# The ninth tap of a split-float32 convolution: 64-row matmuls side by side, or one full-array matmul

## The chip, the cores and the metric

The kernel runs on one core of one Trainium2 chip. The metric is the device time of one execution in microseconds (us); the time before is the median of three runs. A core has TensorE (PE in the profile, with PEld for its weight loads), VectorE (DVE), ScalarE (ACT), GpSimd (POOL) and SyncE (SP). ACT and SP also issue the DMAs of this kernel.

## The reference, cut to what matters

Three layers of one kind, then a fourth of another. `_gn` is a group norm without parameters.

```python
def _L0_conv_ref(inputs, M, Wp, G):          # B,H,W,C = 4,32,32,16; G: (32,32,3,3,16,16)
    first = jnp.einsum('ijpq,bpqc->bijc', M2, inputs)
    K = jnp.transpose(G, (2, 3, 4, 0, 1, 5)).reshape(kh, kw, c, h * w * f)
    shifted = lax.conv_general_dilated(inputs, K, (1, 1), 'SAME', ...)
    shifted = shifted.reshape(b, h, w, h, w, f)
    diff = jax.nn.relu(inputs[:, :, :, None, None, :] - shifted)
    second = jnp.einsum('ijpq,bpqijc->bijc', W2, diff)
    return first - second

x = x + _L0_conv_ref(_gn(x), ...)            # likewise layers 1 and 2
x = x + _L3_conv_ref(_gn(x), ...)            # a 2-D convolution with an impulse response
```

So each layer convolves four 32x32 images of 16 channels with 16384 filters of 3x3x16, one set of 16 filters per output position, subtracts, clips, and sums over all positions with a weight. The convolution is nearly all of the work.

## The kernel before, in words

**Operands.** The products are wanted at float32 accuracy, and PE takes a float32r operand in one pass. Every operand is therefore split exactly into a high piece rounded to float32r and a low remainder, and the four products of the pieces are summed in PSUM. `load_patches` makes `main[0]` (high) and `main[1]` (low): 128 partitions that hold eight of the nine taps times 16 channels, for two image pairs. `load_g` makes `gh` and `gl` of the same 128 rows of the filters. Filters come in 16 chunks per layer, each of `GC` = 8 blocks of 128 columns; a block is 8 output positions times 16 channels.

**The ninth tap** has only 16 rows. `last` holds them eight times over, high and low by turns, and `gn` holds the filters' 16 rows eight times, high in rows 0 to 31 and 64 to 95, low in the others. Rows 0 to 63 thus contain all four products once, and rows 64 to 127 contain them again. Two 64-row matmuls with different images, on the upper and the lower half of the array, each do the whole ninth tap.

**Loops.** A job is one block and one image pair; a layer has 256 jobs. The first 16 take the eight blocks of chunk 0 with pair 0 and then with pair 1; later ones take both pairs of a block in turn. Jobs go two at a time (L311): `main_taps` of the first (16 matmuls of 128 rows and 512 columns, L277), `last_tap` of both (four 64-row matmuls each, L289), `main_taps` of the second. So the array changes between full and 64-row matmuls twice per pair of jobs. A job accumulates into two PSUM tiles of two banks (`pair_psum`, four buffers, all of PSUM). VectorE then takes each tile in one instruction (L301): minimum with zero, times the weights `w`, summed into `acc`.

**Supply.** `next_g` loads the next chunk's filters at the third block of a chunk. ACT issues the DMA of `g` and the eight copies of `g9`, and casts `gh` (L234) and `gn` (L236). POOL subtracts the identity from the middle tap of `g` (L225). VectorE computes `gl` (L235) and the low rows of `gn` (L239, twice). `g` and `g9` have one buffer, `gh`, `gl` and `gn` two, so a chunk's casts wait until PE is through with the chunk two before. SP loads `w`, 1 MB for two blocks, four buffers deep (L254).

**A layer's start.** Group norm on VectorE, `ypad` to DRAM (L140) and back as shifted patches (L158, L167), on SP and ACT by turns; then the first term (L192) with eight loads of `M` (L178), three buffers deep. In layer 0 the impulse response of the last convolution follows on PE, ACT and POOL (L350 to L396). The order of instructions on each engine is set by the framework's scheduler, which also gives each DMA one of eight completion lanes in turn; a DMA waits for the one before it on its lane. [...]

Of the kernel before, what the change touches and what calls it, by code (L numbers as in the profile page):

```python
# [23 lines left out]
F32 = mybir.dt.float32  # L28
F32R = mybir.dt.float32r
AF = mybir.ActivationFunctionType  # L30
ALU = mybir.AluOpType
# [5 lines left out]
B, C, S = 4, 16, 32  # L37
# [3 lines left out]
GC = 8  # L41
# [8 lines left out]
def conv_stack_kernel(ctx, tc, x, M, W, G, den, num, h0, cst, dft, idft, out):  # L50
    nc = tc.nc
# [14 lines left out]
    def pair_psum():  # L66
        return ps.tile([P, 2, 512], F32, tag="pt", name="pt")
# [24 lines left out]
    def group_norm(xt):  # L92

        s = small.tile([P, B], F32, tag="s", name="s")
        nc.vector.tensor_reduce(s, xt, AX.X, ALU.add)
        pm = small_psum()
        nc.tensor.matmul(pm[:, :B], lhsT=avg, rhs=s, start=True, stop=True)
        mean = small.tile([P, B], F32, tag="mean", name="mean")
        nc.vector.tensor_copy(mean, pm[:, :B])
        xc = work.tile([P, B, NBLK], F32, tag="xc", name="xc")  # L100
        nc.vector.tensor_tensor(
            xc, xt, mean.unsqueeze(2).to_broadcast([P, B, NBLK]), ALU.subtract
        )
        sq = work.tile([P, B, NBLK], F32, tag="sq", name="sq")
        nc.vector.tensor_tensor(sq, xc, xc, ALU.mult)
        ss = small.tile([P, B], F32, tag="ss", name="ss")
        nc.vector.tensor_reduce(ss, sq, AX.X, ALU.add)
        pv = small_psum()
        nc.tensor.matmul(pv[:, :B], lhsT=avg, rhs=ss, start=True, stop=True)
        v = small.tile([P, B], F32, tag="v", name="v")  # L110
        nc.vector.tensor_scalar(v, pv[:, :B], 1e-5, None, ALU.add)

        r = small.tile([P, B], F32, tag="r", name="r")
        nc.scalar.activation(r, v, AF.Sqrt)
        ri = small.tile([P, B], F32, tag="ri", name="ri")
        nc.vector.reciprocal(ri, r)
        nc.vector.tensor_tensor(ri, ri, v, ALU.mult)
        nc.vector.tensor_tensor(r, r, ri, ALU.add)
        nc.vector.tensor_scalar(r, r, 0.5, None, ALU.mult)
        rstd = small.tile([P, B], F32, tag="rstd", name="rstd")  # L120
        nc.vector.reciprocal(rstd, r)
        y = work.tile([P, B, NBLK], F32, tag="y", name="y")
        nc.vector.tensor_tensor(  # L123
            y, xc, rstd.unsqueeze(2).to_broadcast([P, B, NBLK]), ALU.mult
        )
        return y
# [85 lines left out]
    def load_g(layer, ch):  # L212

        g = gp.tile([P, GC, P], F32, tag="g", name="g")
        g9 = gp.tile([P, GC, P], F32, tag="g9", name="g9")
        cols = bass.ts(ch, GC * P)
        nc.scalar.dma_start(out=g.rearrange("r n m -> r (n m)"), in_=G[layer][:P, cols])
        for t in range(8):
            nc.scalar.dma_start(
                out=g9[t * C : (t + 1) * C].rearrange("r n m -> r (n m)"),  # L220
                in_=G[layer][P : P + C, cols],
            )

        mid = g[64 : 64 + C].rearrange("r n (p f) -> r (n p) f", f=C)
        nc.gpsimd.tensor_tensor(  # L225
            mid,
            mid,
            ident[64 : 64 + C, 64 : 64 + C].unsqueeze(1).to_broadcast([C, GC * 8, C]),
            ALU.subtract,
        )  # L230
        gh = gs.tile([P, GC, P], F32R, tag="gh", name="gh")
        gl = gs.tile([P, GC, P], F32R, tag="gl", name="gl")
        gn = gs.tile([P, GC, P], F32R, tag="gn", name="gn")
        nc.scalar.copy(gh, g)  # L234
        nc.vector.tensor_tensor(gl, g, gh.bitcast(F32), ALU.subtract)  # L235
        nc.scalar.copy(gn, g9)  # L236
        for r in (32, 96):
            lo = gn[r : r + 32]
            nc.vector.tensor_tensor(lo, g9[r : r + 32], lo.bitcast(F32), ALU.subtract)  # L239
        return gh, gl, gn  # L240

    gt = {}

    def next_g(layer, ch):
        layer, ch = layer + ch // (NBLK // GC), ch % (NBLK // GC)
        if layer < 3 and (layer, ch) not in gt:
            gt[layer, ch] = load_g(layer, ch)

    def load_w(layer, blk):

        cc, q = divmod(blk, S)
        wt = wp.tile([P, 2, S * S], F32, tag="w", name="w")
        src = W[layer][cc, :, q : q + 2, :].rearrange("p k m -> p (k m)")
        nc.sync.dma_start(  # L254
            out=wt.rearrange("p k m -> p (k m)"),
            in_=src.unsqueeze(1).to_broadcast([8, C, 2 * S * S]),
        )
        return wt

    def conv_layer(layer, xt, side=()):  # L260
        y = group_norm(xt)
        main, last = load_patches(y)
        xf = first_term(layer, xt, y)
        for _ in side:
            pass
        acc = work.tile([P, B, NBLK], F32, tag="acc", name="acc")

        jobs = [(blk, a) for a in range(2) for blk in range(GC)]
        jobs += [(blk, a) for blk in range(GC, NBLK) for a in range(2)]
        wt = {}  # L270

        def main_taps(job, tiles, start):
            blk, a = job
            for w in range(2):
                for h in range(2):
                    for t in range(4):
                        nc.tensor.matmul(  # L277
                            tiles[t // 2][:, t % 2, :],
                            lhsT=gt[layer, blk // GC][w][:, blk % GC, :],
                            rhs=main[h][:, a, bass.ts(t % 2, 16), t // 2, :S],  # L280
                            start=start and w == 0 and h == 0,
                            stop=not start and w == 1 and h == 1,
                        )

        def last_tap(job, tiles, start):
            blk, a = job
            for t in range(4):
                rows = slice(64 * (t % 2), 64 * (t % 2) + 64)
                nc.tensor.matmul(  # L289
                    tiles[t // 2][:, t % 2, :],  # L290
                    lhsT=gt[layer, blk // GC][2][rows, blk % GC, :],
                    rhs=last[rows, a, bass.ts(t % 2, 16), t // 2, :S],
                    start=start,
                    stop=not start,
                )

        def second_term(job, tiles):
            blk, a = job
            for t in range(2):
                junk = junkp.tile([P, S * S], F32, tag="junk", name="junk")  # L300
                nc.vector.scalar_tensor_tensor(  # L301
                    junk,
                    tiles[t].rearrange("p h m -> p (h m)"),
                    0.0,
                    wt[blk // 2][:, blk % 2, :],
                    ALU.min,
                    ALU.mult,
                    accum_out=acc[:, 2 * a + t, blk : blk + 1],
                )

        for one, two in zip(jobs[::2], jobs[1::2]):  # L311
            for blk, _ in (one, two):
                if blk % GC == 2:
                    next_g(layer, blk // GC + 1)
                if blk // 2 not in wt:
                    wt[blk // 2] = load_w(layer, blk // 2 * 2)
            p1 = [pair_psum() for _ in range(2)]
            main_taps(one, p1, True)
            p2 = [pair_psum() for _ in range(2)]
            last_tap(one, p1, False)  # L320
            last_tap(two, p2, True)
            main_taps(two, p2, False)
            second_term(one, p1)
            second_term(two, p2)
        xn = xp.tile([P, B, NBLK], F32, tag="x", name="x")
        nc.vector.tensor_tensor(xn, xf, acc, ALU.add)
        return xn
# [80 lines left out]
    def load_toeplitz(k):  # L408

        t = tp.tile([P, C, TQ * PITCH], F32, tag="t", name="t")  # L410
        hv = hd.rearrange("j i t -> i j t")
        for p in range(8):
            at = 8 + k * TQ * PITCH - p
            (nc.sync, nc.scalar)[p % 2].dma_start(
                out=t[p * C : (p + 1) * C], in_=hv[:, :, at : at + TQ * PITCH]
            )
        return t
# [26 lines left out]
    for k in range(S // TQ):  # L444
        t = load_toeplitz(k)
        for q in range(TQ):
            dq = k * TQ + q
            for cc in range(4):
                nc.tensor.matmul(  # L449
                    pov[:, :, 8 * cc :],  # L450
                    lhsT=y3[:, cc, 31 - dq : 31 - dq + S, :].rearrange("p q b -> p (q b)"),
                    rhs=t[:, :, q * PITCH : q * PITCH + S - 8 * cc],
                    start=(dq == 0 and cc == 0),
                    stop=(dq == S - 1 and cc == 3),
# [72 lines left out]
```

## Time and profile before

| | |
|---|---|
| median of 3 runs | 4120.68 us (4115.94 to 4121.74) |
| the profiled execution's own time | 4120.68 us |
| its span | 4119.0 us |
| mean granted TensorE clock | 0.973 (1.00 in the three loops after their first microseconds) |
| PE busy | 3858.6 us, 94% of the span |
| DVE busy | 2102.4 us, 51% |
| the three loops over jobs | about 208 to 1417, 1514 to 2724, 2822 to 4033 us |

The span is what the profiler saw from the first to the last instruction. Lines of groups read: line, engine, operation, output<-input, shapes, count, then busy us and mean ns of one, then the engine's idle time just before these instructions. A matmul's duration reaches from its start to its modelled end and overlaps that of the next, so that rates are to be taken from start times. The chain is the work that ended last, followed back from the end, with the share of the span that each engine or line has in it.

### The profile page before, as it was taken

What the parts mean: (1) busy time and instruction counts of PE and PEld (TensorE: products, weight loads), DVE (VectorE), ACT (ScalarE), POOL (GpSimd) and SP (SyncE); (2) the same over time, 40 slices, a digit from 0 to 9 for tenths busy, and PEclk for the clock granted to TensorE, in tenths of its full rate; (3) what the DMA queues carried; (4) which work ended last, traced back from release to release, by engine and by line L of the source; (5) the groups of instructions that cost most, each with busy time, mean ns of one, the idle gap of its engine ahead of it and who ended that gap; (6) DMA issues with size and microseconds to landing.
All of it is one profiled execution on the core that took longest, in us unless ns stands there. A gap on an engine that the chain in (4) does not pass through costs nothing.

```text
span 4119.0 us, 39252 instructions
## 1 busy us (share of the span) xinstructions
PE 3858.6 (94%) x16164; PEld 2740.8 (67%) x16164; DVE 2102.4 (51%) x3284; ACT 117.0 (3%) x124; POOL 158.7 (4%) x112
## 2 busy tenths in 40 slices
PE   0899999999999759999999999948999999999998
PEld 0577777777777547777777777736777777777775
DVE  0155555555555515555555555532555555555551
ACT  0000000000000000000000000000000000000000
POOL 0400000000000000000000000000000000000000
PEclk9999999999999869999999999977999999999999
DMA  7352232222222362222222222353322222222214
GB/s 144 106 105 70 63 81 62 76 68 68 76 67 67 77 106 72 72 71 65 79 63 71 72 71 62 80 89 60 87 67 69 74 67 67 75 69 63 70 31 67
DMA packets 82401, 305.88 MB, mean 74 GB/s; under 512 B 20589, under 2 KB 37229, under 8 KB 55342
## 3 DMA queue, kind: packets, MB, share of 16 engines
q1 hardware_dynamic: 44414, 224.16, 22.5%
q10 hardware_dynamic: 37808, 79.22, 8.5%
q8 instruction: 127, 2.08, 0.2%
q14 instruction: 52, 0.43, 0.0%
HBM read 300.03 MB, written 3.29 MB: 74 GB/s over the span
## 4 chain that ended last, share of the span: by engine, by line
PE 92%; DMA 5%; POOL 1%; DVE 1%; SPq 0%; issue 0%; ACT 0%; ACTq 0%; DVEq 0%; POOLq 0%
PE pt L277 77%; PE pt L289 11%; DMA main<-img 2%; PE pt L449 2%; DMA w<-in_W_dram 2%; PE pt L192 2%; DMA last<-img 1%; PE pt L386 1%; SPq L140 0%; POOL t L363 0%; DVE junk L301 0%; POOL H L363 0%; DMA mt<-in_M_dram 0%; DMA g<-in_G_dram 0%; DVE gn L239 0%
## 5 line engine op out<-in xcount | busy, mean ns | idle before, releaser
L301 DVE SCALAR_TENSOR_TENSOR junk<-pt,w 128x1024 f32<-128x1024 f32 x1536 | 1880.7, 1224 | 1598.7 <-PE pt L289 888.0
L277 PE MATMUL pt<-main,gh 128*128 128x512 f32 x6144 | 1721.0, 423 | 0.0
L277 PE MATMUL pt<-main,gl 128*128 128x512 f32 x6144 | 1667.0, 415 | 0.0
L277 PEld LDWEIGHTS pt<-main,gh 128*128 128x128 f32 x6144 | 1143.1, 191 | 471.4 <-issue 152.9
L277 PEld LDWEIGHTS pt<-main,gl 128*128 128x128 f32 x6144 | 1174.2, 191 | 368.9
L289 PE MATMUL pt<-last,gn 64*128 64x512 f32 x3072 | 486.1, 436 | 0.0
L289 PEld LDWEIGHTS pt<-last,gn 64*128 64x128 f32 x3072 | 261.1, 186 | 210.8 <-issue 165.5
L192 PE MATMUL pt<-yt,mt 128*128 128x64 f32 x384 | 83.0, 422 | 185.4 <-ACT yt L187 181.1
L225 POOL TENSOR_TENSOR g<-g,cs 16x1024 f32<-16x1024 f32 x48 | 114.1, 2376 | 3632.3 <-DMA g<-in_G_dram 3481.9
L192 PEld LDWEIGHTS pt<-yt,mt 128*128 128x128 f32 x384 | 82.2, 333 | 186.8 <-ACT yt L187 182.3
L236 ACT CAST gn<-g 128x1024 fp32r<-128x1024 f32 x48 | 50.6, 1054 | 3331.2 <-PE pt L289 3325.3
L207 DVE TENSOR_TENSOR xf<-x,pt 128x512 f32<-128x512 f32 x3 | 2.1, 686 | 274.0 <-PE pt L203 274.0
L301 DVE DVE_READ_ACCUMULATOR junk<-pt,w 128x1 f32 x1536 | 127.7, 83 | 0.0
L239 DVE TENSOR_TENSOR gn<-g,gn 32x1024 fp32r<-32x1024 f32 x96 | 117.6, 1225 | 8.6 <-ACT gn L236 5.7
L449 PE MATMUL pt<-t,y 128*128 128x512 f32 (+3 forms) x256 | 72.1, 446 | 1.5 <-DVE y L428 1.5
L449 PEld LDWEIGHTS pt<-t,y 128*128 128x128 f32 x256 | 45.2, 197 | 28.6 <-issue 18.7
L235 DVE TENSOR_TENSOR gl<-g,gh 128x1024 fp32r<-128x1024 f32 x48 | 58.9, 1227 | 8.0 <-ACT gh L234 8.0
L234 ACT CAST gh<-g 128x1024 fp32r<-128x1024 f32 x48 | 50.5, 1051 | 55.3 <-PE pt L277 55.3
L386 PE MATMUL pt<-tb,H 128*128 128x512 f32 (+1 forms) x80 | 40.6, 669 | 8.5 <-ACT sa L356 4.9
L386 PEld LDWEIGHTS pt<-tb,H 128*128 128x128 f32 (+1 forms) x80 | 16.5, 212 | 32.6 <-issue 20.4
L456 DVE TENSOR_TENSOR xo<-xo,pt 128x512 f32<-128x512 f32 x1 | 0.7, 686 | 72.3 <-PE pt L449 72.3
L185 PE MATMUL pt<-cs,y 128*128 128x128 f32 x12 | 3.3, 429 | 24.1 <-DVE y L123 24.1
(58 smaller groups left out, 150.4 us busy)
## 6 DMA issues: line engine op xcount, KB each, us to landing
w<-in_W_dram SPq DMA_DIRECT2D x192, 1024.0 KB
g<-in_G_dram ACTq DMA_DIRECT2D x48, 512.0 KB
g<-in_G_dram ACTq DMA_DIRECT2D x384, 64.0 KB
mt<-in_M_dram ACTq DMA_DIRECT2D x24, 512.0 KB
main<-img ACTq DMA_DIRECT2D x48, 135.9 KB
main<-img SPq DMA_DIRECT2D x48, 135.9 KB
t<-hd SPq DMA_DIRECT2D x32, 160.0 KB
t<-hd ACTq DMA_DIRECT2D x32, 160.0 KB
```

The lines of the kernel that those rows point to most:

```text
L185: nc.tensor.transpose(py[:, bass.ts(b, P)], y[:, b, :], ident)
L192: nc.tensor.matmul(pf[:, bass.ts(pn, B * C)], lhsT=mt[:, pm, :], rhs=yt[:, pm].rearrange("k b c -> k (b c)"), start=(pm == 0), stop=(pm == 7),
L225: nc.gpsimd.tensor_tensor(mid, mid, ident[64 : 64 + C, 64 : 64 + C].unsqueeze(1).to_broadcast([C, GC * 8, C]), ALU.subtract,)
L234: nc.scalar.copy(gh, g)
L235: nc.vector.tensor_tensor(gl, g, gh.bitcast(F32), ALU.subtract)
L236: nc.scalar.copy(gn, g9)
L239: nc.vector.tensor_tensor(lo, g9[r : r + 32], lo.bitcast(F32), ALU.subtract)
L277: nc.tensor.matmul(tiles[t // 2][:, t % 2, :], lhsT=gt[layer, blk // GC][w][:, blk % GC, :], rhs=main[h][:, a, bass.ts(t % 2, 16), t // 2, ...
L289: nc.tensor.matmul(tiles[t // 2][:, t % 2, :], lhsT=gt[layer, blk // GC][2][rows, blk % GC, :], rhs=last[rows, a, bass.ts(t % 2, 16), t // ...
L301: nc.vector.scalar_tensor_tensor(junk, tiles[t].rearrange("p h m -> p (h m)"), 0.0, wt[blk // 2][:, blk % 2, :], ALU.min, ALU.mult, accum_ ...
L386: nc.tensor.matmul(ph[ij], lhsT=H[:nf, ch, ri, bass.ts(ij, P)], rhs=tb[:nf], start=(ch == 0 and ri == 0), stop=(ch == len(FCH) - 1 and ri ...
L449: nc.tensor.matmul(pov[:, :, 8 * cc :], lhsT=y3[:, cc, 31 - dq : 31 - dq + S, :].rearrange("p q b -> p (q b)"), rhs=t[:, :, q * PITCH : q ...
```

## The change

The ninth tap's products are put on 64 of the 128 rows of one full-array matmul. In `load_g`, `g9` is loaded four times instead of eight; `gn` has its high and low rows in 0 to 63 only, and rows 64 to 127 are set to zero by POOL. In the loop, the pairing of jobs goes: each job runs five terms of four full-array matmuls, the fifth being `gn` with `last`. `last` itself is loaded as before, all 128 rows.

```diff
@@ load_g
-        for t in range(8):
+        for t in range(4):
             nc.scalar.dma_start(
                 out=g9[t * C : (t + 1) * C].rearrange("r n m -> r (n m)"),
...
-        nc.scalar.copy(gn, g9)
-        for r in (32, 96):
-            lo = gn[r : r + 32]
-            nc.vector.tensor_tensor(lo, g9[r : r + 32], lo.bitcast(F32), ALU.subtract)
+        nc.scalar.copy(gn[:64], g9[:64])
+        lo = gn[32:64]
+        nc.vector.tensor_tensor(lo, g9[32:64], lo.bitcast(F32), ALU.subtract)
+        nc.gpsimd.memset(gn[64:].bitcast(F32), 0.0)
@@ conv_layer
-        def main_taps(job, tiles, start):
...
-        def last_tap(job, tiles, start):
-            blk, a = job
-            for t in range(4):
-                rows = slice(64 * (t % 2), 64 * (t % 2) + 64)
-                nc.tensor.matmul(
-                    tiles[t // 2][:, t % 2, :],
-                    lhsT=gt[layer, blk // GC][2][rows, blk % GC, :],
-                    rhs=last[rows, a, bass.ts(t % 2, 16), t // 2, :S],
...
-            p1 = [pair_psum() for _ in range(2)]
-            main_taps(one, p1, True)
-            p2 = [pair_psum() for _ in range(2)]
-            last_tap(one, p1, False)
-            last_tap(two, p2, True)
-            main_taps(two, p2, False)
-            second_term(one, p1)
-            second_term(two, p2)
+        for blk, a in jobs:
...
+            gh, gl, gn = gt[layer, blk // GC]
+            pt = [pair_psum() for _ in range(2)]
+            terms = [(gh, main[0]), (gh, main[1]), (gl, main[0]), (gl, main[1]), (gn, last)]
+            for k, (w, im) in enumerate(terms):
+                for t in range(4):
+                    nc.tensor.matmul(
+                        pt[t // 2][:, t % 2, :],
+                        lhsT=w[:, blk % GC, :],
+                        rhs=im[:, a, bass.ts(t % 2, 16), t // 2, :S],
+                        start=k == 0,
+                        stop=k == len(terms) - 1,
+                    )
             for t in range(2):
...
                 nc.vector.scalar_tensor_tensor(
```

The VectorE instruction per tile is the same as before.

More of the change, by code (lines that the diff above doesn't have):

```diff
@@ L270, in conv_layer @@
         wt = {}
-        def main_taps(job, tiles, start):
-            blk, a = job
-            for w in range(2):
-                for h in range(2):
-                    for t in range(4):
-                        nc.tensor.matmul(
-                            tiles[t // 2][:, t % 2, :],
[L279 to L283, printed above, removed]
-        def last_tap(job, tiles, start):
-            blk, a = job
-            for t in range(4):
-                rows = slice(64 * (t % 2), 64 * (t % 2) + 64)
-                nc.tensor.matmul(
-                    tiles[t // 2][:, t % 2, :],
-                    lhsT=gt[layer, blk // GC][2][rows, blk % GC, :],
-                    rhs=last[rows, a, bass.ts(t % 2, 16), t // 2, :S],
[L293 to L298, printed above, removed]
+        for blk, a in jobs:
+            if blk % GC == 2:
+                next_g(layer, blk // GC + 1)
+            if blk // 2 not in wt:
+                wt[blk // 2] = load_w(layer, blk // 2 * 2)
+            gh, gl, gn = gt[layer, blk // GC]
[10 more added lines that the diff above has]
+                    )
             for t in range(2):
@@ L302, in second_term @@
                     junk,
-                    tiles[t].rearrange("p h m -> p (h m)"),
+                    pt[t].rearrange("p h m -> p (h m)"),
                     0.0,
@@ L309, in second_term @@
                 )
[L311 to L316, printed above, removed]
-            p1 = [pair_psum() for _ in range(2)]
-            main_taps(one, p1, True)
-            p2 = [pair_psum() for _ in range(2)]
-            last_tap(one, p1, False)
-            last_tap(two, p2, True)
-            main_taps(two, p2, False)
-            second_term(one, p1)
-            second_term(two, p2)
         xn = xp.tile([P, B, NBLK], F32, tag="x", name="x")
```

## The prediction

> **What bounds the kernel now.** I read the page's busy table and its chain first, to see which engine sets the end; then the groups, for durations; then the timeline of one period in mid-loop, because the means of pipelined matmuls overlap and only start times give a rate.
>
> ```profile
> span 4119.0 us, 39252 instructions
> PE 3858.6 (94%) x16164; PEld 2740.8 (67%) x16164; DVE 2102.4 (51%) x3284; ACT 117.0 (3%) x124; POOL 158.7 (4%) x112
> PE 92%; DMA 5%; POOL 1%; DVE 1%; SPq 0%; issue 0%; ACT 0%; ACTq 0%; DVEq 0%; POOLq 0%
> ...
> L277 PE MATMUL pt<-main,gh 128*128 128x512 f32 x6144 | 1721.0, 423 | 0.0
> L289 PE MATMUL pt<-last,gn 64*128 64x512 f32 x3072 | 486.1, 436 | 0.0
> ```
>
> PE is 92% of the chain, and its two matmul groups sat idle before them for 0.0 us: nothing but PE's own rate holds the loops. The mean of 423 ns is a latency, not a rate, as 12288 matmuls at 423 ns would exceed the span. The rate is in the timeline, PE alone (start, duration, line, count):
>
> ```profile
> 2001.64 1.27 PE L289 MATMUL pt<-last,gn 64*128 64x512 f32 x8
> 2002.84 2.29 PE L277 MATMUL pt<-main,gh 128*128 128x512 f32 x8
> 2004.96 2.17 PE L277 MATMUL pt<-main,gl 128*128 128x512 f32 x8
> 2006.97 2.19 PE L277 MATMUL pt<-main,gh 128*128 128x512 f32 x8
> 2008.99 2.17 PE L277 MATMUL pt<-main,gl 128*128 128x512 f32 x8
> 2011.08 0.77 PE L289 MATMUL pt<-last,gn 64*128 64x512 f32 x4
> ```
>
> One period is two jobs: L289 starts at 2001.64 and again at 2011.08, 9.44 us. Three layers of 128 pairs give 384 x 9.44 = 3625 us; the three loops by their own edges (208 to 1417, 1514 to 2724, 2822 to 4033) are 3630. The other 489 us are layer starts, the impulse response and the last convolution.
>
> Within the period, 16 full-array matmuls lie between 2004.96 and 2008.99: **251.9 ns** each. The start at 2006.97 is a job boundary, with its new PSUM tiles, and it costs nothing. The 32 full-array matmuls take 2011.08 - 2002.84 = 8.24 us, against 32 x 0.2519 = 8.06: 0.18 us is lost at the edges of the run. The eight 64-row matmuls take 1.20 us, 150 ns each; as two row halves side by side they would need 4 slots, 1.01 us, so 0.19 us more is lost there.
>
> **What the Trainium skill says.** "TensorEngine Tiling (Array Packing)", Key Properties: changing the tiling mode drains TensorE. The trace agrees: 0.18 + 0.19 = 0.37 us for the two changes of a period. "TensorE: Matmul & The Clock Gate", the closing goals table: a matmul on few rows takes as long as one on 128, and the gain is that tiles run at once. The trace agrees (150 ns each in pairs, 252 alone). The same page, Part 2, Phases on the wall clock: a warm gap of 215.7 ns for 512 columns. The trace differs (251.9), and I use the trace. "SBUF - State Buffer", Who interferes with whom: a VectorE instruction with two SBUF inputs contends with a GpSimd one that reads SBUF, not with one that only writes. The trace fits the first half (L239 at most 1639 ns against a median of 1220, while L301, one input in PSUM, never above 1226); no run here shows the second.
>
> **The change on PE.** The ninth tap's 64-row matmuls go (two to a slot), and each job has four full-array ones in their place, half of whose rows multiply zeros. Per pair of jobs: minus 1.20 us (eight 64-row matmuls with a mode change), minus 0.18 us (the edges of the 32-run), plus 8 x 0.2519 = 2.015 us. That is **+0.636 us**, a period of 40 x 0.2519 = 10.076 us, and 384 times that is **+244 us**. All of it is on the path. LDWEIGHTS stays hidden: one per matmul in both kernels, 191 ns on 128 rows and 186 on 64. Bounds on the rate: below, 250.0 ns, as the first pairs of each layer have it (9.38 us periods at 1529.84); above, 254.5, as far over the steady figure. They make +215 and +284 us.
>
> **Edits beside the path.** Four copies of the ninth tap's rows per chunk are no longer loaded: 192 issues of about 0.4 us, 77 us of ACT's queue, and 12 MB. The L236 cast on 64 partitions rather than 128 should keep its 1.05 us. One L239 subtraction per chunk goes: 48 x 1.22 = 59 us of DVE. A POOL memset of 64x1024 per chunk comes: the nearest row is a memset of 128x1008 at 0.94 us, so 45 us. I count all at nothing, as ACT, DVE and POOL are busy 97, 2045 and 102 us of the loops' 3630 while PE does not wait for them. If that cover were gone, the bill is at most 59 us gained and 45 lost.
>
> The memset waits until PE has read the old gn. Behind it on POOL stands the next chunk's correction of g, which ACT's cast waits for; but that waits for its DMA anyway (3481.9 us of idle in 44 waits, 72.9 us each), about 5 us after a chunk ends, and the memset is over after 1.
>
> **PSUM's ring is the new slack to watch.** Both kernels have four double-bank tiles; now every job takes two. A job's tiles are wanted back 5.04 us after its end. VectorE needs two L301 of 1.23 us, 1.34 apart. In the built order, at a chunk's end gl stands before the job's first L301 and gn between the two. With the cast of gn ending 1.2 us after the job, the second L301 ends near 4.2 us. The second tile is wanted at 5.5. I take no stall; the slack is 1.3 us.
>
> **Layer 0's start moves too**, though the diff doesn't touch it: the scheduler has put things in another order. The chain of waits before:
>
> ```profile
> 9.89 14.25 DMA w<-in_W_dram
> 24.16 31.08 DMA w<-in_W_dram
> 55.61 0.42 SPq L140
> ...
> 61.85 6.53 DMA main<-img
> ```
>
> The fourth w load shares a completion lane with the first, lands at 55.24, and SP's third store of ypad waits for that lane. In the new order only three w loads stand ahead of the stores, on lanes that SP's stores don't use; the fourth comes after the patches. Also ahead of the patches are one M load instead of three and four g9 copies instead of eight: 1.0 + 1.0 + 0.25 = 2.25 MB less. At the 143 GB/s of the first 110 us that is 16 us. ACT's square root now stands ahead of the casts, so y comes at about 12 us, not 28. I let the patch loads begin near 44 instead of 61.85: minus 17 us. Two M loads (4.1 us each from issue to landing) and the fourth w then compete with the first term: plus 5. Net **-12 us**, from -22 (nothing given back) to +3 (all of the moved bytes exposed). The impulse response's chain behind it, POOL and PE from 135 to 208, keeps its length.
>
> At layers 1 and 2, gn's cast and subtraction fall after the last L301 but one: plus 0.5 us each. The correction of g may no longer stretch the square (2.71 us beside it, 0.69 alone), and 0.25 MB less is loaded: together **-1 us**, between -6 and +5.
>
> **Sum.** 4119.0 + 244 - 12 - 1 = 4350 us of span. The profiled execution's own time is 4120.68 for that span, 1.7 more, and it is also the median of the three runs: **4352 us**, +5.6%.
>
> **Rivals.** (1) *The ring stalls.* If a GpSimd read holds VectorE's gl or gn for the 2.4 us of the correction of g, the slack of 1.3 us is gone and PE waits up to 1.1 us at each of 45 chunks, 50 us: 4400. Against it: the correction comes 5 us after the chunk's end. (2) *The dense stream is slower.* The first eight full-array matmuls after a mode change take 2.12 us, 265 ns each; if a stream without pauses settled at 257, that is 15360 x 5 ns = 78 us: 4430. Against it: 24 in a row at 252 show no trend. (3) *It ends faster.* The mode changes could be what keeps LDWEIGHTS from being fetched ahead, so that a stream without them runs at the skill's 215.7 ns. The new period would be 8.63 us and the time 4352 - 15360 x 36 ns, about 3796. It decides from 236 ns on (9.44 / 40). Against it: the rate within a run of 32 is flat, and far from the edges it should already be the undisturbed one. (4) *It doesn't do what it says*: the 64-row matmuls were not side by side, so eight full ones cost no more than those. Then only the drains would go, 384 x 0.37 = 142 us gained. The 150 ns excludes it: that is below one slot.
>
> **How the numbers follow.** The main case 0.82, with 4325 to 4385 as its own range; ring 0.06; slower stream 0.07; faster 0.04; within the bound 0.01. About 0.2% (8 us) is what a measurement of this kernel can tell from no change. The range of 4322 to 4392 holds the main case with its bounds and some of the ring's; what it leaves out is the two tails. Faster 0.04, same 0.01, slower 0.95.
>
> **What would show it.** In the new profile: 15360 matmuls at one line, job starts 5.04 us apart, no 64-row form, PE's idle before them near zero, and the first loop matmul near 196 us instead of 207.8. A job period under 4.72 us would make me wrong in sign; one with a gap ahead of the gh matmuls, with DVE as the releaser, points to the ring; an even one above 5.1 us, to the rate.

## The result and the profile after

The changed kernel takes 4339.19 us (median of four runs, 4335.3 to 4342.56) beside 4121.21 for the kernel before: 1.0531 times as long, 95% interval 1.0512 to 1.0549. The forecast was 4352, with a range of 4322 to 4392. The profiled execution has a span of 4340.8 us, 221.8 more than before.

The page after: busy table, chain by engine, and the groups that answer to those of before.

```profile
span 4340.8 us, 39012 instructions
PE 4079.0 (94%) x16164; PEld 3095.7 (71%) x16164; DVE 2046.2 (47%) x3236; ACT 115.5 (3%) x123; POOL 203.8 (5%) x160
PE 93%; DMA 6%; POOL 1%; DVE 0%; issue 0%; ACTq 0%; ACT 0%; SPq 0%; DVEq 0%; POOLq 0%
L280 PE MATMUL pt<-main,gh 128*128 128x512 f32 x6144 | 1667.1, 415 | 0.0
L280 PE MATMUL pt<-main,gl 128*128 128x512 f32 x6144 | 1665.9, 415 | 0.0
L280 PE MATMUL pt<-last,gn 128*128 128x512 f32 x3072 | 899.1, 415 | 0.0
L238 POOL MEMSET gn<- 64x1024 f32 x48 | 45.5, 947 | 3619.1 <-PE pt L280 3619.0
L235 ACT CAST gn<-g 64x1024 fp32r<-64x1024 f32 x48 | 50.4, 1049 | 88.7 <-PE pt L280 88.7
L237 DVE TENSOR_TENSOR gn<-g,gn 32x1024 fp32r<-32x1024 f32 x48 | 58.5, 1220 | 1.5
```

PE is 93% of the chain, and its three groups were idle before them for 0.0 us: no stall has come in. The ninth tap is now 128*128, and its group has grown from 486.1 to 899.1 us with the same count. Note that PE's "94%" is the same in both kernels, while one is 5% slower. The share says who sets the end, not how well it is used.

The timeline of the changed kernel, PE alone in mid-loop:

```profile
2004.27 1.16 PE L280 MATMUL pt<-last,gn 128*128 128x512 f32 x4
2005.27 2.17 PE L280 MATMUL pt<-main,gh 128*128 128x512 f32 x8
2007.27 2.17 PE L280 MATMUL pt<-main,gl 128*128 128x512 f32 x8
2009.28 1.18 PE L280 MATMUL pt<-last,gn 128*128 128x512 f32 x4
```

One job runs from 2004.27 to 2009.28: 5.01 us for 20 matmuls, 250.5 ns each, and nothing is lost at the passage from one term to the next. Two jobs take 10.02 us where they took 9.44.

Where the 221.8 us are, by the first and last loop matmul of each layer in both traces (a last end is its group's last start row plus duration):

| part | before | after | difference |
|---|---|---|---|
| start to first loop matmul | 207.8 | 206.6 | -1 |
| three loops | 1209.7 + 1210.5 + 1210.0 | 1282.9 + 1284.1 + 1284.0 | +221 |
| two passages between layers | 96.6 + 98.1 | 98.5 + 98.5 | +2 |

The last convolution's part agrees to a fraction of a microsecond.

### The profile page after: what moved, and what is told of

Its sections match the earlier page's. It is cut to its first block, busy times and chain, and to the rows that moved or that the text cites. A ratio compares the mean times of both kernels' runs of the same rounds, so it can differ in the third digit from the quotient of the medians.

```text
span 4340.8 us, 39012 instructions
## 1 busy us (share of the span) xinstructions
PE 4079.0 (94%) x16164; PEld 3095.7 (71%) x16164; DVE 2046.2 (47%) x3236; ACT 115.5 (3%) x123; POOL 203.8 (5%) x160
## 4 chain that ended last, share of the span: by engine, by line
PE 93%; DMA 6%; POOL 1%; DVE 0%; issue 0%; ACTq 0%; ACT 0%; SPq 0%; DVEq 0%; POOLq 0%
PE pt L280 89%; DMA main<-img 2%; PE pt L422 2%; PE pt L191 2%; DMA w<-in_W_dram 1%; DMA last<-img 1%; PE pt L359 1%; DMA mt<-in_M_dram 1%; ACTq L139 0%; POOL t L336 0%; DVE junk L289 0%; DMA img<-ypad 0%; DMA tb<-in_idft_dram 0%; DMA img<-zrow 0%; POOL H L336 0%
## 5 line engine op out<-in xcount | busy, mean ns | idle before, releaser
L280 PE MATMUL pt<-main,gh 128*128 128x512 f32 x6144 | 1667.1, 415 | 0.0
L280 PEld LDWEIGHTS pt<-main,gh 128*128 128x128 f32 x6144 | 1174.3, 191 | 367.4 <-ACT hs L369 0.8
L280 PE MATMUL pt<-last,gn 128*128 128x512 f32 x3072 | 899.1, 415 | 0.0
L280 PEld LDWEIGHTS pt<-last,gn 128*128 128x128 f32 x3072 | 586.8, 191 | 183.3
L238 POOL MEMSET gn<- 64x1024 f32 x48 | 45.5, 947 | 3619.1 <-PE pt L280 3619.0
L237 DVE TENSOR_TENSOR gn<-g,gn 32x1024 fp32r<-32x1024 f32 x48 | 58.5, 1220 | 1.5
L235 ACT CAST gn<-g 64x1024 fp32r<-64x1024 f32 x48 | 50.4, 1049 | 88.7 <-PE pt L280 88.7
```

The costliest lines, as they stand in the source:

```text
L235: nc.scalar.copy(gn[:64], g9[:64])
L237: nc.vector.tensor_tensor(lo, g9[32:64], lo.bitcast(F32), ALU.subtract)
L238: nc.gpsimd.memset(gn[64:].bitcast(F32), 0.0)
L280: nc.tensor.matmul(pt[t // 2][:, t % 2, :], lhsT=w[:, blk % GC, :], rhs=im[:, a, bass.ts(t % 2, 16), t // 2, :S], start=k == 0, stop=k == ...
```

## The experiments

Times of the kernel before beside these runs were 4121.9 us (first four) and 4117.24 us (last four). The theory was that the loops follow PE's slots and its changes of array form, and nothing else; the rivals were the order of jobs, the PSUM ring, and a price that belongs to the 64-row matmuls themselves.

**Four changes of form per pair instead of two.** The kernel before, with each job's last tap after its own main taps:

```diff
             p1 = [pair_psum() for _ in range(2)]
             main_taps(one, p1, True)
-            p2 = [pair_psum() for _ in range(2)]
             last_tap(one, p1, False)
-            last_tap(two, p2, True)
-            main_taps(two, p2, False)
+            p2 = [pair_psum() for _ in range(2)]
+            main_taps(two, p2, True)
+            last_tap(two, p2, False)
```

> The kernel before, with the same matmuls, but each job's four 64-row matmuls directly after its own 16 full-array ones: four changes of array form per pair of jobs in place of two. My theory (a change of form costs 0.18 to 0.19 us by itself): period 9.44 + 0.37 = 9.81 us, 384 x 0.37 = +142 us, 4263. Rival (the lost time belongs to the 64-row matmuls themselves, or to any run of full ones, not to the change): no difference, 4121.

Measured: 4262.62 us, 1.0346 times before (1.033 to 1.0361). Its timeline in mid-loop:

```profile
2002.44 2.27 PE L277 MATMUL pt<-main,gh 128*128 128x512 f32 x8
2004.55 2.16 PE L277 MATMUL pt<-main,gl 128*128 128x512 f32 x8
2006.64 0.77 PE L289 MATMUL pt<-last,gn 64*128 64x512 f32 x4
2007.33 2.28 PE L277 MATMUL pt<-main,gh 128*128 128x512 f32 x8
```

The 16 full-array matmuls take 4.20 us (16 x 0.2519 is 4.03), the four 64-row ones 0.69 (two slots are 0.50). So 0.17 and 0.19 us, 0.36 us together, are lost for the two changes of each job, where the kernel before loses 0.37 us for the two changes of a pair of jobs: the same price, paid twice as often with the same instructions. It belongs to the change of form.

**The full-array ninth tap in the old order.** The kernel before, with the new `load_g` (four copies, zeros in rows 64 to 127) and

```diff
-                rows = slice(64 * (t % 2), 64 * (t % 2) + 64)
+                rows = slice(0, P)
```

> The ninth tap on the full array as in the changed kernel, but in the pair order of the kernel before (main, both last taps, main; VectorE after both). My theory (the array form is all that counts, not the order of jobs): 4339, as the changed kernel, with 250.4 ns per matmul. Rival (the order or the PSUM ring has a share): nearer to 4121, or a rate of 251.9 ns as in the kernel before, that is 4362.

Measured: 4344.22 us, 1.0542 (1.0525 to 1.056), beside 1.0531 for the changed kernel. The medians are 5 us apart. From the first to the last loop matmul of each layer, the three loops take 3860 us here, 3851 in the changed kernel and 3630 in the kernel before: the order of jobs, VectorE's turn after two jobs instead of one, and the use of the ring are worth 9 us together, and the array form carries the rest. In the timeline 32 matmuls take 8.03 us (2000.91 to 2008.94), 250.9 ns each, although the order is that of before; a pair of jobs takes 10.04 us.

```profile
2000.91 2.19 PE L277 MATMUL pt<-main,gh 128*128 128x512 f32 x8
2002.93 2.17 PE L277 MATMUL pt<-main,gl 128*128 128x512 f32 x8
2004.93 2.16 PE L289 MATMUL pt<-last,gn 128*128 128x512 f32 x8
2006.93 2.18 PE L277 MATMUL pt<-main,gh 128*128 128x512 f32 x8
2008.94 2.17 PE L277 MATMUL pt<-main,gl 128*128 128x512 f32 x8
2010.95 2.19 PE L277 MATMUL pt<-main,gh 128*128 128x512 f32 x8
2012.97 2.17 PE L277 MATMUL pt<-main,gl 128*128 128x512 f32 x8
```

**No ninth tap.** The changed kernel without its fifth term:

```diff
-            terms = [(gh, main[0]), (gh, main[1]), (gl, main[0]), (gl, main[1]), (gn, last)]
+            terms = [(gh, main[0]), (gh, main[1]), (gl, main[0]), (gl, main[1])]
```

> The changed kernel without the ninth tap's matmuls (this leaves the ninth tap out of the result; its loads and casts stay). My theory (four slots of 250.4 ns per job, all on the path): 4339 - 768 x 4 x 0.2504 = 3570. Rival (the ring of PSUM tiles or VectorE at 2.7 us per job takes over in part): above 3620.

Measured: 3577.25 us, 0.8681 (0.8664 to 0.8699). Four matmuls per job are worth (4339.2 - 3577.3) / 3072 = 248 ns each: the price of a slot is paid in full, and with jobs of 4 us VectorE still does not set the time. The ninth tap, 16 of 144 rows of each product, costs 18% of the changed kernel.

**64 rows without a partner.** The changed kernel with the fifth term on rows 0 to 63 alone:

```diff
-                        lhsT=w[:, blk % GC, :],
-                        rhs=im[:, a, bass.ts(t % 2, 16), t // 2, :S],
+                        lhsT=w[: 64 if k == 4 else P, blk % GC, :],
+                        rhs=im[: 64 if k == 4 else P, a, bass.ts(t % 2, 16), t // 2, :S],
```

> The changed kernel with its ninth-tap matmuls on rows 0 to 63 alone: same number, order and data, 64-row form without a partner. My theory (a lone 64-row matmul takes a full slot, and each job has two changes of form at 0.18 to 0.19 us): period 5.01 + 0.37 = 5.38 us, 4339 + 284 = 4623. Rival (the form costs nothing without a second tile in use): 4339.

Measured: 4639.56 us, 1.126 (1.1237 to 1.1282), the slowest of all. Its timeline:

```profile
2004.99 1.26 PE L280 MATMUL pt<-last,gn 64*128 64x512 f32 x4
2006.18 2.27 PE L280 MATMUL pt<-main,gh 128*128 128x512 f32 x8
2008.29 2.17 PE L280 MATMUL pt<-main,gl 128*128 128x512 f32 x8
2010.38 1.28 PE L280 MATMUL pt<-last,gn 64*128 64x512 f32 x4
```

Four lone 64-row matmuls take 1.19 us, against 0.69 side by side, and the job takes 5.39 us instead of 5.01. Half the rows save nothing; only the partner does. So the zeros that the change multiplies are free as such. What the change lost is the partner, and what it gained is that the two changes of form per pair of jobs are gone.

**Both kernels with less work.** The low-by-low product of the eight main taps is left out, in the kernel before and in the changed one:

```diff
# before
-            for w in range(2):
-                for h in range(2):
+            for w, h in ((0, 0), (0, 1), (1, 0)):
...
-                            stop=not start and w == 1 and h == 1,
+                            stop=not start and w == 1,
# changed
-            terms = [(gh, main[0]), (gh, main[1]), (gl, main[0]), (gl, main[1]), (gn, last)]
+            terms = [(gh, main[0]), (gh, main[1]), (gl, main[0]), (gn, last)]
```

> The kernel before without the low-by-low product of the eight main taps (gl with main[1]); the ninth tap keeps all four. Twelve full-array matmuls per job instead of 16, side-by-side 64-row matmuls as before. My theory (period = 24 x 0.2519 + 0.18 + 1.20 = 7.43 us in place of 9.44): 4121 - 384 x 2.015 = 3347. Rival (VectorE's 5.4 us per pair and the PSUM ring begin to hold PE): above 3400.

> The changed kernel without the same low-by-low product: 16 full-array matmuls per job. My theory: 4339 - 768 x 4 x 0.2504 = 3570, so that the change costs as many us on this base (about +225) as on the full one (+218). Rival (part of the change's price is VectorE's or the ring's, and grows when PE has less to do): over +260 between the two.

Measured: 3353.58 us (0.8144, 0.8132 to 0.8156) and 3575.57 us (0.8684, 0.8669 to 0.8698). The difference between the forms is 222 us, and 218 with all products: it does not change when PE has a fifth less to do. The first of them is faster than both kernels of this study, at the price of one of the four products. Its timeline shows the old structure with shorter runs, a period of 7.44 us:

```profile
2001.51 1.26 PE L288 MATMUL pt<-last,gn 64*128 64x512 f32 x8
...
2008.95 1.26 PE L288 MATMUL pt<-last,gn 64*128 64x512 f32 x8
```

**M loads early.** The changed kernel, with the first three M loads of each layer ahead of the group norm:

```diff
+        mts = [load_m(layer, pn) for pn in range(3)]
         y = group_norm(xt)
         main, last = load_patches(y)
-        xf = first_term(layer, xt, y)
+        xf = first_term(layer, xt, y, mts)
...
-            mt = load_m(layer, pn)
+            mt = mts[pn] if pn < len(mts) else load_m(layer, pn)
```

> The changed kernel with the first three M loads of each layer written ahead of the group norm, so that in layer 0 three of them (and, by the scheduler's order, the fourth w load) stand ahead of the patches again; the loops are untouched. Theory A (the new order's gain at layer 0's start was given back by M loads in the first term): first term 33 us long instead of 41, patches start near 55 to 62 instead of 47; first loop matmul again at 205 to 209 us. Theory B (the two are separate, and early M loads are a clear gain): first loop matmul near 198.

One run, 4333.78 us. The timelines of layer 0's start, first the changed kernel, then this one (patch loads, end of the patches, first term, its end):

```profile
47.14 10.81 ACTq L157 DMA_DIRECT2D main<-img  x8
92.56 0.58 ACT L186 COPY yt<-pt 128x512 f32<-128x512 f32 x1 [77.56 <-DMA main<-img]
102.13 3.67 PE L191 MATMUL pt<-yt,mt 128*128 128x64 f32 x16 [5.25 <-DMA mt<-in_M_dram]
134.08 0.58 ACT L199 COPY ft<-pt 128x512 f32<-128x512 f32 x1 [40.93 <-PE pt L191]
```

```profile
62.31 11.78 ACTq L157 DMA_DIRECT2D main<-img  x8
107.11 0.58 ACT L186 COPY yt<-pt 128x512 f32<-128x512 f32 x1 [87.93 <-DMA last<-img]
107.75 27.38 PEld L191 LDWEIGHTS pt<-yt,mt 128*128 128x128 f32 x128 [86.06 <-ACT yt L186]
135.36 0.58 ACT L199 COPY ft<-pt 128x512 f32<-128x512 f32 x1 [8.34 <-PE pt L191]
```

With the M loads early the patches start 15 us later, the first term has no gap and is 13 us shorter (28 us, where theory A had 33), and it ends within 1.3 us of the same point (134.08 and 135.36). That is theory A in kind: the wait moved and the end stayed. It is not a test of the M loads alone, as the fourth w load and the second chunk's g also went ahead of the patches. The first loop matmul came at 202.75 instead of 206.6, outside the span given for A by 2 us, but this is no gain that the run shows: four traces with the changed kernel's own order of loads (its own, the full-array ninth tap's, its run with less work, and that with neighbouring elements) have it at 206.6, 205.4, 202.0 and 203.2.

**Neighbouring elements.** The changed kernel, with another reading of the images:

```diff
-                        rhs=im[:, a, bass.ts(t % 2, 16), t // 2, :S],
+                        rhs=im[:, a].rearrange("p r b x -> p (r b x)")[:, 512 * t : 512 * t + 512],
```

> The changed kernel with every moving operand of the loops read as 512 neighbouring elements instead of 16 pieces of 32 (this makes the convolution another one). Theory A (the 250 ns per matmul hold about 37 ns for the pieces): about 216 ns, 4339 - 15360 x 0.034 = 3810. Theory B (the rate is set by the weight load or the pairing of load and matmul): 250 ns, 4339.

One run, 4057.43 us. In its timeline 20 matmuls take 4.64 us, 232 ns each:

```profile
2002.04 1.09 PE L280 MATMUL pt<-last,gn 128*128 128x512 f32 x4
2002.97 2.02 PE L280 MATMUL pt<-main,gh 128*128 128x512 f32 x8
2004.83 2.01 PE L280 MATMUL pt<-main,gl 128*128 128x512 f32 x8
2006.68 1.08 PE L280 MATMUL pt<-last,gn 128*128 128x512 f32 x4
```

Neither theory: 18 of the 250 ns go with this reading, and 232 are left. Why those are more than the 215.7 ns that the prediction cites from the Trainium skill stays open. A form of both kernels that reads neighbouring elements and still computes the convolution was not run.

## Why the prediction was right, and where it was off

**The path and the arithmetic held.** PE alone sets the loops, four slots per pair of jobs become eight, and the changes of form go. Each of the three prices was shown by a run of its own: the change of form (four changes: 4263 expected, 4262.62 measured), the slot (no ninth tap: 3570 and 3577.25), and the partner (lone 64 rows: 4623 and 4639.56).

**The loops' term was 10% too large: +244 against +221.** The step that was off is the 251.9 ns that I carried from the mixed stream into the pure one. It measured 250.5. Over 15360 matmuls 1.4 ns are 21 us, and that is nearly all of it. The low bound of 250.0 ns had it inside. The changes of form are not what slowed the sixteen matmuls of the sample: with the full-array ninth tap in the old order, where no change is left, the same places of the period (`gl` of the second job and `gh` of the next, 2008.94 to 2012.97) take 4.03 us, again 251.9 ns each, while eight of the first job's `gl` and eight of the ninth tap take 2.00 us, 250 ns each. The sample was the slower part of a stream that averages less. That run's 32 main matmuls take 8.04 us (6.04 from 2006.93 to 2012.97, and 2.00 from 2002.93), against 8.24 in the kernel before, so that the edges of a run cost 0.20 us rather than 0.18.

**Luck in the sum.** The loops were put 23 us too high, and the two other terms together 14 us too low, so that the misses partly cancel in the 4352. Either one alone would still have left the result in the range.

**Figures that do not come out of the prediction's own numbers.** The upper rate of 254.5 ns is 2.6 over the steady one, not "as far over" as 250.0 is under it; that would be 253.8, and +273 instead of +284. For layer 0's start "nothing given back" is -17, not -22, and nothing shows how +3 was reached. The 44 waits of the correction of g average 79 us; 72.9 is a common value. And the 252 ns "alone" were of full-array matmuls: the trace before has no lone 64-row matmul in its loops, so only the run without a partner shows that one takes a full slot.

**Layer 0's start was to gain 12 us and gained 1.** The first half of the reading was right in kind: SP's stores no longer wait for the fourth w load, and the patch loads begin at 47.1 (44 was forecast, 61.85 before). But they then take ACT 45.4 us to issue, where they took 41.4, so that the patches' end is 9 us earlier rather than 17. And the first term lasts from 92.56 to 134.08, 41.5 us, where it lasted 32.9: the give-back was 8.6 us, not 5. The run with early M loads fits one account of both, in which the stage passes nearly the same bytes in either order. The upper bound of +3, "all of the moved bytes exposed", was the right description: by the end of the first term the DMAs had moved 19.3 MB before and 18.9 after, at means of 144 and 141 GB/s. The 1 us is no measurement of this order of loads, as the same point varies more from execution to execution: 204.0 to 208.7 in three traces with the order of before, 202.0 to 206.6 in four with that of the changed kernel.

**The passages between layers: +2 instead of -1.** At the first one the correction of g fell beside the layer's closing addition, which took 2.75 us instead of 0.69, and no longer beside the square, which took 0.69 instead of 2.71; that cancels. The 2 us are in the patches: from the first cast of `ypad` to the copy of `yt` they took 53.8 us before (1430.63 to 1484.42) and 55.4 after (1503.04 to 1558.44). At the second passage they took 1.8 us longer too, and the group norm ahead of them 1.4 less. Why the patches take longer is not shown.

**What was counted at nothing cost nothing.** The memset takes 947 ns (0.94 forecast), the cast on half the partitions keeps its 1.05 us, VectorE lost 56 us of work (59 forecast), and PE's idle before the loops' matmuls is 0.0 us. At the end of a chunk the ring stood as worked out. The changed kernel's timeline at such an end in mid-loop, VectorE and POOL:

```profile
1989.50 1.23 DVE L234 TENSOR_TENSOR gl<-g,gh 128x1024 fp32r<-128x1024 f32 x1 [2.04 <-ACT gh L233]
1990.48 0.95 POOL L238 MEMSET gn<- 64x1024 f32 x1 [73.83 <-PE pt L280]
1990.64 1.22 DVE L289 SCALAR_TENSOR_TENSOR junk<-pt,w 128x1024 f32<-128x1024 f32 x1
1991.90 1.21 DVE L237 TENSOR_TENSOR gn<-g,gn 32x1024 fp32r<-32x1024 f32 x1
1993.14 1.23 DVE L289 SCALAR_TENSOR_TENSOR junk<-pt,w 128x1024 f32<-128x1024 f32 x1
1994.38 2.39 POOL L224 TENSOR_TENSOR g<-g,cs 16x1024 f32<-16x1024 f32 x1 [2.94 <-DVE junk L289]
```

The job's last matmul ends at 1990.42 and its second tile is free at 1994.4, 3.9 us later (4.2 forecast, 5.5 allowed). The correction of g follows 4.0 us after the chunk's end, where 5 was forecast, and just clear of the last of these instructions. The memset overlaps gl, which has two SBUF inputs, for 0.24 us (0.59 in two of the chunks), and no gl so overlapped took over 1.23 us. That is the half of the Trainium skill's sentence that the trace before could not show ("SBUF - State Buffer", Who interferes with whom): a GpSimd instruction that only writes does not hold VectorE.

**The rivals.** The ring did not stall, and the dense stream was not slower than the mixed one. The faster case wanted a slot below 236 ns and gave the changes of form as what stands in its way; without them the slot is 250.5 ns, which refutes it. The 232 ns of neighbouring elements do not speak for it: they have another cause, and that reading was not tried in the kernel before. That the 64-row matmuls were not side by side is refuted by 0.69 us for four of them against 1.19.

## What to carry to other kernels

Count PE's work in slots: here a 64-row matmul of 512 columns takes a full slot like one of 128 rows, and half a slot only where two row halves run side by side. Then charge every change of array form, here some 0.19 us or three quarters of a slot. Side by side pays when the saved slots outweigh the changes: in this kernel 4 saved slots (1.0 us) against 2 changes (0.37 to 0.39 us) per pair of jobs, 0.58 us net by the two periods, and with a change after every job still 77 us better than the full array. At a start that waits for DMA, ask how many bytes must pass before the stage ends. Here some were sent later, and the wait moved with them: the first term ended at 134.6 us before and 134.1 after.

## What the runs showed that was not expected

A float32r matmul of 512 columns, one record each in the trace (15360 for 768 jobs of 20), does not run at one rate: 232 ns with neighbouring elements, 250.0 to 251.9 on average with 16 pieces of 32. The pieces do not cost the same everywhere. The four matmuls of a term take the two halves of the pair's first image (t = 0, 1), then those of the second (t = 2, 3). In the changed kernel a term's four and the next one start at 2005.27, 2005.51, 2005.74, 2006.01 and 2006.27. Over the loops' steady part the mean time to the next start is 238 and 229 ns for the first image and 264 and 271 for the second; with neighbouring elements, in the same places of PSUM, all four have 232 to 233. So the 18 ns are not a price of pieces as such: the first image's matmuls, also in pieces, run near the rate without them. Why the second image's are slower is not shown. (By the same indices the 64-row partners are the two halves of one image, t = 0 with 1 and t = 2 with 3, and not different images as the description of the kernel before has it.)

The image pair matters a little as well. In the changed kernel the first jobs of a layer, all with image pair 0, take 5.00 us, those with pair 1 take 5.03, and from the 17th on, by turns, 5.01; by the program the two pairs differ only in their data and in where they lie in the tile.
